# The returning products of the last two experts as seven products of 2x2 blocks

## The chip, the cores and the metric

The program runs on one core of one Trainium2 chip. The metric is the time of one execution on the device, in microseconds (us); less is better. All data is float32.

## The reference, cut to what matters

Two layers stand one behind the other. The first has a recurrent attention with a gated feed-forward part beside it; the second has a latent attention with 16 heads and a mixture of four experts beside it, and both parts of a layer add to its input `x`. The change touches the four experts alone:

```python
def _L1_ffn_ref(x, gate_up_proj, down_proj):      # x: 8 x 512 x 512 seen as 2048 rows of 512
    x4 = x.reshape(B, G, E, H)                    # E = 4: row j*4 + e goes to expert e
    gu = jnp.einsum('bgeh,ehd->bged', x4, gate_up_proj)
    gate, up = (gu[..., :I], gu[..., I:])
    inter = jax.nn.silu(gate) * up                # I = 512
    out = jnp.einsum('bgei,eih->bgeh', inter, down_proj)   # the returning product
    return out.reshape(B, N, H)
```

For each expert the returning product is a matrix of 512 tokens x 512 gated features times one of 512 x 512, added to the residual `y`.

## The kernel before, in words

The kernel has three parts in this order: the first layer (up to about 969 us of the profiled execution), the four experts (969 to 1135 us) and the latent attention (1135 us to the end). Each engine works through its own instructions in order. In the first and second part a scheduler sets that order from the program's dependences; instructions that go through `pin` (most of the attention's, and `fold`'s) keep the order in which they are written.

**Hidden products.** For each expert `hidden(e)` (L985) computes gate and up products. It already does so by seven products of 2x2 blocks: `right_sums(e)` (L947) makes four sums of the expert's tokens in the tile `t_ops` (four slots of 128x512), `left_sums` (L955) three sums of the weights in the tile `s_ops` and one in the weights' own place; the products are matmuls 256 columns wide (L969) into the PSUM tiles `epg` and `epu`, ScalarE copies partial results into `hold`, and the gated result goes to the tile `inter` (L1018), 128 x 4 x 512: gated features on the partitions, four chunks of them, by 512 tokens.

**Returning products.** `returned(e)` (L1024) takes, for each of four batches of 128 tokens, four matmuls of 128x512 (one for each chunk of gated features) into one PSUM bank `epo` of the pool `psp` (two banks), and VectorE adds the bank to `y` (L1039). The weights are the tile `dn`, loaded by `downs` (L921) through SyncE's queue while the expert before is returned. The order is: `hidden(1)`, `returned(0)`, `hidden(2)`, `returned(1)`, `hidden(3)`, `returned(2)` (L1062), `returned(3)` (L1082). Between them, in the second and third of these, the scheduler sets the preparation of the attention's first weights (`fold`, L850).

**What follows.** The attention's first instructions are the key and query products of its first head, `pk` (L1116) and `pq` (L1124), in the PSUM pool `ps_pj` (L1090), which takes over the experts' banks. Then ScalarE adds the bias, VectorE turns the vectors (`rotate`, L1094, instructions of L1099 and L1105) and GpSimd ends the turning (L1109); only then come the scores (L1134).

**The shared tiles.** `s_ops` and `t_ops` live through experts and attention. The attention's output product is by seven block products as well; its right sums (`right_operands`, L1219, four instructions of GpSimd on L1222 to L1225) are written to `t_ops`. In GpSimd's queue they stand ahead of two loads of rows of `W_O` (L859) and of all instructions of L1109.

**A matmul in the trace.** A float32 matmul shows as two records, so the 32 matmuls of 128x512 of `returned(2)` and `returned(3)` are 64 records, and they overlap: a record's duration is longer than the distance between two of them.

Of the kernel before, what the change touches and what calls it, by code (L numbers as in the profile page):

```python
# [12 lines left out]
F32 = mybir.dt.float32  # L13
# [5 lines left out]
P = 128  # L19
# [32 lines left out]
E, EI = 4, 512  # L52
# [3 lines left out]
def trunk_kernel(ctx: ExitStack, tc: tile.TileContext, a: dict, out: bass.AP):  # L56
    nc = tc.nc
# [48 lines left out]
    with ExitStack() as px:  # L106
# [303 lines left out]
        def queries_out(n, wh):  # L410

            po = ps_st.tile([P, NC, 4, K + 1], F32, tag="pso", name=f"pso_{n}")
            for be in range(NC):
                for b, r in enumerate(quarters):
                    mm(po[r, be, :, :K], wh[:, 4 * b + be, :], wq_bd[:, 4 * b + be, :, HD:], be == 0, False)
            return po
# [364 lines left out]
        for n in range(NM):  # L781
            wh = weights_out(n)
            pz = first_product(n, pre)
            po = queries_out(n, wh)
# [25 lines left out]
    y = [ypool.tile([P, E, HS], F32, tag=f"y{b}", name=f"y{b}") for b in range(B)]  # L810
    lat = ctx.enter_context(tc.tile_pool(name="lat", bufs=1, reuse_waits="tile"))
    ckv = lat.tile([P, B, L], F32, tag="ckv", name="ckv")
    s_ops = lat.tile([P, 3, 2, L // 2], F32, tag="s_ops", name="s_ops")
    t_ops = lat.tile([P, 4, 2, HS // 2], F32, tag="t_ops", name="t_ops")
# [24 lines left out]
    def batch_latents(hg, b):  # L839
        t = lat.tile([P, QC // P, L], F32, tag="cq", name=f"cq_{hg}_{b}", bufs=2)  # L840
        for i in range(QC // P):
            nc.sync.dma_start(out=t[:, i], in_=lat_d[1 + i][:, b].rearrange("p k x -> p (k x)"))
        return t

    def group_tiles(pool, hg):
        w = {nm: pool.tile([P, HPG, D], F32, tag=nm, name=f"{nm}_{hg}", bufs=1) for nm in ups}
        w["vo"] = pool.tile([P, HPG, HS], F32, tag="vo", name=f"vo_{hg}", bufs=1)
        return w
# [53 lines left out]
    with ExitStack() as px:  # L902
# [4 lines left out]
        psp = px.enter_context(tc.tile_pool(name="d_ps", bufs=2, space=PSUM))  # L907
        ps_gu = px.enter_context(tc.tile_pool(name="d_psgu", bufs=2, space=PSUM))
# [3 lines left out]
        def fetch(**kw):  # L912

            tc.keep_in_program_order(nc.sync.dma_start(**kw))
# [6 lines left out]
        def downs(e):  # L921
            dn = wd.tile([P, EI // P, HS], F32, tag="dn", name=f"dn_{e}")
            fetch(out=dn, in_=a["dn"][e].rearrange("(c p) o -> p c o", p=P))
            return dn
# [10 lines left out]
        dns = {0: downs(0)}  # L935
# [3 lines left out]
        half = B * P // 2  # L939
# [3 lines left out]
        def tokens(e, c, h):  # L943

            return xe[:, NCHUNK * h : NCHUNK * (h + 1), 2 * c : 2 * c + 2, e, :].rearrange("p k c j -> p c k j")

        def right_sums(e):  # L947
            t1, t2, t3, t4 = (t_ops[:, n].rearrange("p c (k j) -> p c k j", k=NCHUNK) for n in range(4))
            b22 = tokens(e, 1, 1)
            nc.vector.tensor_sub(t1, tokens(e, 0, 1), tokens(e, 0, 0))  # L950
            nc.vector.tensor_sub(t2, b22, t1)
            nc.vector.tensor_sub(t3, b22, tokens(e, 0, 1))
            nc.vector.tensor_sub(t4, tokens(e, 1, 0), t2)
# [29 lines left out]
        inters = {}  # L983
# [40 lines left out]
        def returned(e):  # L1024

            dn, inter = dns.pop(e), inters.pop(e)
            if e + 1 < E:
                dns[e + 1] = downs(e + 1)
            for b in range(B):
                po = psp.tile([P, HS], F32, tag="po", name=f"epo_{e}_{b}")  # L1030
                for i in range(EI // P):
                    nc.tensor.matmul(  # L1032
                        po,
                        lhsT=inter[:, i, b * P : (b + 1) * P],
                        rhs=dn[:, i, :],
                        start=(i == 0),
                        stop=(i == EI // P - 1),
                    )
                nc.vector.tensor_add(y[b][:, e, :], po, y[b][:, e, :])  # L1039

        right_sums(0)
        for e in range(E):
            if e == 1:
                nc.gpsimd.memset(ones, 1.0)
                nc.sync.dma_start(out=wqr, in_=a["W_QR"])
                nc.sync.dma_start(out=wkr, in_=a["W_KR"])
                buv16 = wk.tile([H, D], F32, tag="sg", name="buv16")
                nc.sync.dma_start(out=buv16, in_=a["b_UV"].rearrange("(h d) -> h d", d=D))
                w0 = group_tiles(lat, 0)
                cqs = {(0, 0): batch_latents(0, 0)}  # L1050
                first = fold(w0, 0, wk, lambda nm: psp.tile([P, 512], F32, tag="pa", name=nm), 1)
                nc.sync.dma_start(out=buk, in_=a["b_UK"])
                nc.sync.dma_start(out=buq, in_=a["b_UQ"])
                for k in range(E):
                    nc.sync.dma_start(
                        out=trig_k[RD:, :].rearrange("p (k e j) -> p k e j", k=NCHUNK, e=E)[:, :, k],
                        in_=a["trig"][:, k * P : (k + 1) * P].rearrange("p (k j) -> p k j", k=NCHUNK),
                    )
                nc.sync.dma_start(out=ckv, in_=lat_d[0].rearrange("p b k x -> p b (k x)"))
            hidden(e)  # L1060
            if e > 0:
                returned(e - 1)  # L1062
            if e in (1, 2):
                next(first, None)
            if e == 2:

                for wr, bias in ((wkr, buk), (wqr, buq)):
                    pb = psp.tile([P, 512], F32, tag="pa", name="pb")
                    nc.tensor.matmul(pb[RD:, :H], lhsT=wr, rhs=bias, start=True, stop=True)
                    nc.vector.tensor_copy(bias[RD:, :], pb[RD:, :H])  # L1070
                pb = psp.tile([P, 512], F32, tag="pa", name="pbuv")
                nc.tensor.transpose(pb[:, :H], buv16, ident[:H, :H])
                nc.vector.tensor_copy(buv, pb[:, :H])
                nc.vector.tensor_scalar_mul(buq[:RD, :], buq[:RD, :], scale)
                tc.keep_in_program_order(nc.vector.tensor_scalar_mul(trig_q[RD:, :], trig_k[RD:, :], scale))
            if e == 2:
                for b in range(B):
                    pt = psp.tile([P, E, P], F32, tag="pa", name=f"lv_tr_{b}")
                    for k in range(E):
                        nc.tensor.transpose(pt[:, k, :], ckv[:, b, k * P : (k + 1) * P], ident)  # L1080
                    nc.scalar.copy(lv[:, b], pt)
        returned(E - 1)  # L1082

# [2 lines left out]
    with ExitStack() as px:  # L1088
# [123 lines left out]
        half = L // 2  # L1212
# [109 lines left out]
        for i in range(nu + 1):  # L1322
# [37 lines left out]
            k = i - (nu - HPG * B)  # L1360
            if 0 <= k < HPG * B:
                b, e = divmod(k, HPG)
# [4 lines left out]
        po = {}  # L1367
# [106 lines left out]
```

## Time and profile before

| what | us |
|---|---|
| three executions, timed | 2035.77, 2028.45, 2035.72 |
| their median | 2035.72 |
| the profiled execution, its own time | 2030.29 |
| its span, first to last instruction | 2028.3 |
| TensorE busy in the span | 1968.2 (97%) |
| VectorE, ScalarE, GpSimd busy | 1302.3, 863.2, 631.8 |
| from the last hidden products of the last expert to the attention's first product, 1106.0 to 1135.5 | 29.5, of it TensorE 28.72, VectorE 7.91, ScalarE 1.01, GpSimd 4.02 |
| the 64 records of `returned(2)` and `returned(3)` in it, first and last start | 1106.23, 1134.1 |

The three timed executions lie 7.3 us apart, and the profiled one lies between them. About 2 us of its own time lie around its span.

In the profile's rows PE is TensorE, PEld its weight loads, DVE VectorE, ACT ScalarE, POOL GpSimd, and SPq the queue of SyncE. A row of the timeline gives the start in us, the time from the first start to the last end, the engine, the line, the operation, the tile written and those read, the shape, and in brackets how long the engine sat idle before it and what ended that. Rows of equal instructions that follow each other are merged (x62).

### The profile page before, as it was taken

The page shows a single profiled execution, that of the slowest core. Times are in us where ns is not written, and L with a number is a line of the kernel's source. Part 1 is how long each engine was busy: PE and PEld are TensorE (multiplying, and loading weights), DVE is VectorE, ACT ScalarE, POOL GpSimd, SP SyncE. Part 2 cuts the span into 40 slices and gives each one's busy share as a digit, 9 for nine tenths or more (in the row PEclk, how much of TensorE's full clock was granted, in tenths as well). Part 3 has the DMA queues.
Part 4 walks back from the last instruction along what each step waited for, and adds up shares of the span by engine and source line. Part 5 has one row for each costly group of instructions (what it writes and reads, how often), then busy time and mean ns, then how long its engine had stood idle before and what let it go on. Part 6 is the DMA issues. An engine that isn't in the chain of part 4 may idle for free.

```text
span 2028.3 us, 30787 instructions
## 1 busy us (share of the span) xinstructions
PE 1968.2 (97%) x10502; PEld 1245.2 (61%) x10502; DVE 1302.3 (64%) x2720; ACT 863.2 (43%) x1763; POOL 631.8 (31%) x707
## 2 busy tenths in 40 slices
PE   8999999999999999998999999999999999999999
PEld 6777676767676776744776445555555555555555
DVE  4546657575756574754654487777777777777773
ACT  2233343333343443422322365555555555555552
POOL 4334242434342433421001132223223232354320
PEclk9999999999999999999999999999999999999999
DMA  6757576646373655545831144344434443333332
GB/s 166 210 129 220 132 193 166 183 128 184 114 203 116 179 151 163 182 136 189 281 104 56 39 101 117 95 103 115 108 94 114 103 114 86 97 97 89 94 100 93
DMA packets 318472, 270.90 MB, mean 134 GB/s; under 512 B 87660, under 2 KB 239405, under 8 KB 317677
## 3 DMA queue, kind: packets, MB, share of 16 engines
q1 hardware_dynamic: 298080, 237.31, 43.2%
q0 software_dynamic: 8736, 26.31, 4.5%
q10 hardware_dynamic: 11500, 5.32, 0.9%
q8 instruction: 84, 1.38, 0.3%
q14 instruction: 72, 0.58, 0.1%
HBM read 174.18 MB, written 34.87 MB: 103 GB/s over the span
## 4 chain that ended last, share of the span: by engine, by line
PE 47%; DVE 1%; SPq 1%; ACT 1%; issue 0%; DMA 0%; DVEq 0%; ACTq 0%
PE sc L1134 9%; PE pc L1202 9%; PE pq L1124 7%; PE px L1245 5%; PE p L1245 4%; PE epg L969 3%; PE epo L1032 3%; PE pk L1116 2%; PE epu L969 1%; SPq L1194 1%; PE po L1302 1%; PE pw L868 1%; PE pvo L886 1%; ACT prob L1139 1%; ACT prob L1144 0%
## 5 line engine op out<-in xcount | busy, mean ns | idle before, releaser
L1139 ACT ACTIVATE prob<-sc,mx 128x512 f32<-128x512 f32 x256 | 174.3, 683 | 164.2 <-DVE mx L1136 159.4
L1134 PE MATMUL sc<-kT,qT 96*128 96x512 f32 x512 | 230.6, 592 | 1.6 <-DVE prT_head L1183 1.3
L1202 PE MATMUL pc<-prT,lv 128*128 128x512 f32 x488 | 219.6, 593 | 1.2 <-DMA prT<-tt 1.2
L1109 POOL TENSOR_TENSOR kT<-t_k,t_k 32x512 f32<-32x512 f32 x64 | 80.6, 1259 | 407.6 <-PE pq L1124 235.6
L1163 DVE STREAM_TRANSPOSE tt<-prob 128x512 f32<-128x512 f32 x248 | 170.3, 706 | 55.2 <-ACT prob L1144 43.7
L117 PE MATMUL pf<-xT,wg 128*128 128x256 f32 x704 | 173.7, 388 | 5.3 <-DMA wg<-in_wg 2.7
L1144 ACT ACTIVATE prob<-prob,sm 128x512 f32<-128x512 f32 x256 | 176.5, 713 | 0.0
L1124 PE MATMUL pq<-cq,uq 128*128 128x512 f32 x384 | 175.3, 592 | 0.8 <-ACT ctxT L1204 0.8
L1134 PEld LDWEIGHTS sc<-kT,qT 96*128 96x128 f32 x512 | 96.8, 190 | 124.1 <-issue 118.9
L1136 DVE TENSOR_REDUCE mx<-sc 128x1 f32<-128x512 f32 x256 | 168.0, 677 | 2.3 <-PE sc L1134 0.3
L117 PE MATMUL pf<-xT,wu 128*128 128x256 f32 x704 | 167.0, 380 | 1.3 <-DMA wu<-in_wu 1.3
L117 PE MATMUL pd<-wd,hid 128*128 128x512 f32 x352 | 165.9, 600 | 1.8 <-DMA wd<-in_wd 1.7
L117 PEld LDWEIGHTS pf<-xT,wg 128*128 128x128 f32 x704 | 132.1, 192 | 32.9 <-issue 7.6
L1202 PEld LDWEIGHTS pc<-prT,lv 128*128 128x128 f32 x488 | 92.5, 190 | 93.7 <-issue 90.7
L117 PEld LDWEIGHTS pf<-xT,wu 128*128 128x128 f32 x704 | 133.7, 190 | 20.4 <-DMA wu<-in_wu 2.3
L478 DVE SCALAR_TENSOR_TENSOR hid<-pf,us,sg 128x256 f32<-128x256 f32 x88 | 41.9, 477 | 153.9 <-ACT sg L477 153.5
L1124 PEld LDWEIGHTS pq<-cq,uq 128*128 128x128 f32 x384 | 72.8, 190 | 93.1 <-issue 81.5
L314 POOL TENSOR_SCALAR sk<-k,m 128x256 f32<-128x256 f32 x64 | 61.1, 964 | 179.8 <-PE pz L117 167.7
L421 POOL TENSOR_SCALAR gh<-grad,m 128x256 f32<-128x256 f32 x64 | 61.2, 967 | 153.2 <-DVE grad L390 135.5
L117 PEld LDWEIGHTS pd<-wd,hid 128*128 128x128 f32 x352 | 63.4, 190 | 60.5 <-issue 45.2
L1109 POOL TENSOR_TENSOR qT<-t_q,t_q 32x512 f32<-32x512 f32 x64 | 80.6, 1260 | 56.7 <-DVE t_q L1105 56.6
L477 ACT ACTIVATE sg<-pf,gs 128x256 f32<-128x256 f32 x88 | 41.5, 473 | 132.9 <-PE pf L117 132.5
(304 smaller groups left out, 3546.6 us busy)
## 6 DMA issues: line engine op xcount, KB each, us to landing
prT<-tt SPq DMA_DIRECT2D x992, 64.0 KB, 2.0
wd<-in_wd SPq DMA_DIRECT2D x176, 256.0 KB, 3.0
wg<-in_wg SPq DMA_DIRECT2D x88, 256.0 KB, 3.1
wu<-in_wu SPq DMA_DIRECT2D x88, 256.0 KB, 3.1
cq<-lat_d SPq DMA_DIRECT2D x48, 256.0 KB, 4.3
rows<-rows SPq DMA_DIRECT2D x128, 66.0 KB, 2.2
kv<-rows POOLq DMA_DIRECT2D x32, 264.0 KB, 4.1
gu<-in_gu SPq DMA_DIRECT2D x3, 2048.0 KB, 8.8
```

The lines of the kernel that those rows point to most:

```text
L117: nc.tensor.matmul(out, lhsT=lhsT, rhs=rhs, start=start, stop=stop, skip_group_check=True)
L421: nc.gpsimd.tensor_scalar_mul(gh[:, :, h, :], g, m2[:, h : h + 1])
L969: nc.tensor.matmul(ps, lhsT=w[:, c, :], rhs=x[:, c], start=start and c == 0, stop=c == 1, skip_group_check=True)
L1109: nc.gpsimd.tensor_sub(t[RD:mid, :], t1[RD:mid, :], t2[RD:mid, :])
L1124: nc.tensor.matmul(pq, lhsT=w[f"uq{i}"][:, h, :], rhs=cqs[hg, b][:, i, :], start=(i == 0), stop=(i == nq - 1))
L1134: pin(nc.tensor.matmul(ps, lhsT=qT[:KQ, i * P : (i + 1) * P], rhs=kT[:KQ, :], start=True, stop=True))
L1136: pin(nc.vector.tensor_reduce(mx, ps, AX.X, ALU.max, negate=True))
L1139: pin(nc.scalar.activation(pr, ps, AF.Exp, bias=mx, scale=1.0, accum_out=sm))
L1144: pin(nc.scalar.mul(pr, pr, sm))
L1163: nc.vector.transpose(out=tt[:, :, :, i, :], in_=pr.rearrange("p (kb e j) -> p kb e j", e=2, j=K))
L1202: pin(nc.tensor.matmul(pc, lhsT=lv[:, b, k, :], rhs=prT[:, k, :], start=(k == 0), stop=(k == E - 1)))
L1245: nc.tensor.matmul(ps[:, q, :], lhsT=a[:, k, q * P : (q + 1) * P], rhs=w[:, k, :], start=start and k == 0 and q == 0, stop=k == 1, skip_gr ...
```

## The change

For the experts 2 and 3 `returned` gives way to a new function; the experts 0 and 1 keep the old one. With the gated features cut in two halves (k) and the tokens and the output columns in two halves each, the product of two 2x2 block matrices is made with seven block products instead of eight, at the price of eight sums of blocks before them. Each block product is four matmuls, 256 columns wide. Four of the seven gather in one bank `x`, which VectorE reads between two of them, since the partial sums there are outputs themselves.

```diff
+        def returned_by_blocks(e):
+            dn, inter = dns.pop(e), inters.pop(e)
+            if e + 1 < E:
+                dns[e + 1] = downs(e + 1)
+            a11, a12, a21, a22 = (inter[:, 2 * k : 2 * k + 2, q * half : (q + 1) * half] for q in range(2) for k in range(2))
+            b11, b12, b21, b22 = (dn[:, 2 * k : 2 * k + 2, o : o + half] for k in range(2) for o in (0, half))
+            s1, s2, s4 = (s_ops[:, n] for n in range(3))
+            t1, t2, t3, t4 = (t_ops[:, n] for n in range(4))
+            nc.vector.tensor_sub(t1, b12, b11)
+            nc.vector.tensor_sub(t2, b22, t1)
+            nc.vector.tensor_add(s1, a21, a22)
+            nc.vector.tensor_sub(s2, s1, a11)
+            nc.vector.tensor_sub(t3, b22, b12)
+            nc.vector.tensor_sub(a21, a11, a21)
+            nc.vector.tensor_sub(s4, a12, s2)
+            nc.vector.tensor_sub(t4, b21, t2)
+
+            def product(ps, w, x, start=True):
+                for k in range(2):
+                    for q in range(2):
+                        nc.tensor.matmul(
+                            ps[:, q, :],
+                            lhsT=w[:, k, q * P : (q + 1) * P],
+                            rhs=x[:, k, :],
+                            start=start and k == 0 and q == 0,
+                            stop=k == 1,
+                            skip_group_check=True,
+                        )
+
+            def add(ps, qh, oh):
+                for q in range(2):
+                    t = y[2 * qh + q][:, e, oh * half : (oh + 1) * half]
+                    nc.vector.tensor_add(t, ps[:, q, :], t)
+
+            def bank(nm):
+                return psp.tile([P, 2, half], F32, tag="po", name=f"{nm}_{e}")
+
+            x = ps_gu.tile([P, 2, half], F32, tag="pg", name=f"eox_{e}")
+            product(x, a11, b11)
+            add(x, 0, 0)
+            p2 = bank("eo2")
+            product(p2, a12, b21)
+            product(x, s2, t2, False)
+            add(p2, 0, 0)
+            add(x, 0, 1)
+            p5 = bank("eo5")
+            product(p5, s1, t1)
+            product(x, a21, t3, False)
+            add(p5, 0, 1)
+            add(p5, 1, 1)
+            add(x, 1, 1)
+            p3 = bank("eo3")
+            product(p3, s4, b22)
+            product(x, a22, t4, False)
+            add(p3, 0, 1)
+            add(x, 1, 0)
...
             if e > 0:
-                returned(e - 1)
+                (returned if e < E - 1 else returned_by_blocks)(e - 1)
...
-        returned(E - 1)
+        returned_by_blocks(E - 1)
```

The sums are VectorE's, 128x512 each; they use the tiles that the hidden products and, later, the attention's output use: `s_ops`, `t_ops` and, for `a21`, the expert's own `inter`. The bank `x` is one of the hidden products' two `epg` banks; the other three products share the two `epo` banks.

## Prediction

> **What bounds the kernel now.** I read the page first, then the busy times by stage, then the timelines of TensorE, VectorE and GpSimd around the two returning products. The page says that TensorE bounds the whole:
>
> ```profile
> PE 1968.2 (97%) x10502; PEld 1245.2 (61%) x10502; DVE 1302.3 (64%) x2720; ACT 863.2 (43%) x1763; POOL 631.8 (31%) x707
> ```
>
> The stage of the change, by the windows (TensorE, weight loads, VectorE, ScalarE, GpSimd, then clock and DMA):
>
> ```profile
> 1107.95:1135.51 27.56, 26.77 (x64) 11.59 (x62) 6.79 (x12) 0.63 (x1) 2.31 (x3) 1.00 0.22 63
> ```
>
> TensorE is without a pause at full clock (1.00); VectorE has 6.79 us of work in 27.56. What ends here is TensorE's row, and one hand-over behind it. TensorE's timeline:
>
> ```profile
> 1104.40 1.13 PE L969 MATMUL epu<-xe,s_ops 128*128 128x256 f32 x4
> 1105.37 1.03 PE L969 MATMUL epg<-t_ops,gu 128*128 128x256 f32 x4
> 1106.23 1.02 PE L1032 MATMUL epo<-dn,inter 128*128 128x512 f32 x2
> 1107.09 1.03 PE L969 MATMUL epg<-t_ops,gu 128*128 128x256 f32 x4
> 1107.95 26.77 PE L1032 MATMUL epo<-dn,inter 128*128 128x512 f32 x62
> 1135.51 1.12 PE L1116 MATMUL pk<-ckv,uk 128*128 128x512 f32 x2 [0.79 <-DVE y L1039]
> ```
>
> Four records of 256 columns start 0.86 us before the next group (1105.37 to 1106.23), so 0.2155 us each; 62 of 512 columns give (26.77 - 0.592) / 61 = 0.429 each (0.592 is one record's mean). The last line shows the hand-over: `pk` waits for VectorE's last addition. VectorE's timeline there, and three of its rows elsewhere:
>
> ```profile
> 1058.59 0.69 DVE L950 TENSOR_TENSOR t_ops<-xe 128x512 f32<-128x512 f32 x1
> 1059.19 0.42 DVE L961 TENSOR_TENSOR s_ops<-gu 128x256 f32<-128x256 f32 x1
> 1059.53 0.69 DVE L951 TENSOR_TENSOR t_ops<-xe,t_ops 128x512 f32<-128x512 f32 x1
> ...
> 1134.76 0.69 DVE L1039 TENSOR_TENSOR y<-epo,y 128x512 f32<-128x512 f32 x1 [2.74 <-PE epo L1032]
> ```
>
> A sum of 128x512 lasts 0.69 us, but the next starts 0.60 behind it (1058.59, 1059.19); one of 128x256 lasts 0.42, the next starts 0.34 behind (1059.19, 1059.53). A result is read 0.20 us after TensorE's slot ends (slots end at 1107.95 + 62 x 0.429 = 1134.56, the addition starts at 1134.76), and TensorE starts 0.06 after an addition's end (1135.45, 1135.51).
>
> **The change part by part.**
>
> *TensorE.* Removed: 32 matmuls of 128x512, 64 records x 0.429 = 27.47 us. Added: 2 experts x 7 products x 4 matmuls = 56 of 128x256, 112 records x 0.2155 = 24.14 us. Gain 3.33 us. The price of 0.2155 is that of the same shape with its own weight load (190 ns) for each record, as in the hidden products. Nothing else of TensorE's is in the stretch, so the gain counts in full unless TensorE has to wait.
>
> *The last hand-over.* Before, `pk` starts 0.95 us after the last slot (1134.56 to 1135.51). In the built program of the changed kernel it waits for the additions of `eo3` of the last expert, and four matmuls (1.72 us) into `x` stand behind those products. Addition ready after 0.20 + 0.34 + 0.42 + 0.06 = 1.02 us: hidden with 0.70 to spare. Gain 0.95 us; if the cover went, it would cost what it cost before.
>
> *The sums and additions.* Removed from VectorE: 8 additions of 128x512. Added: 16 sums of 128x512 and 28 additions of 128x256. At the distances above, 16 x 0.60 + 28 x 0.34 = 19.1 us in a stretch of 24.1, so VectorE is at 80% and can make TensorE wait. I walked the built program's order through with these distances, from TensorE's slot at 1105.37 and VectorE free at 1103.81. `t1` and `s1` start when the last hidden products have read `t_ops` and `s_ops` (1103.54 + 0.20); the sums of expert 2 stand among the last operations of `hidden(3)` and end at 1109.7. TensorE needs none of them before it has done a11·b11, the last hidden product and a12·b21, at 1110.54; then it takes half of s1·t1, and at 1111.40 it is to add to `x`, which VectorE must have read by then:
>
> | TensorE comes to `x` for | at | VectorE is through with it | to spare |
> |---|---|---|---|
> | expert 2, s2·t2 | 1111.40 | 1111.13 | 0.27 |
> | expert 2, a21·t3 | 1114.42 | 1114.15 | 0.27 |
> | expert 2, a22·t4 | 1117.87 | 1117.57 | 0.30 |
> | expert 3, s2·t2 | 1123.47 | 1123.42 | 0.05 |
> | expert 3, a21·t3 | 1126.49 | 1126.22 | 0.27 |
> | expert 3, a22·t4 | 1129.51 | 1129.23 | 0.28 |
>
> Between two products into `x` the scheduler has put three other matmuls (1.29 us) or more, against the 1.02 that a reading takes, so where VectorE is free the pause is covered. The first and the fourth line are queues of VectorE: all eight sums of expert 2 stand ahead of the first reading, and six of expert 3 between the additions ahead of the fourth, where only 0.05 is left. Sum: no wait, `pk` at 1131.23 in place of 1135.51, **4.28 us** less. Cost of the sums from both sides: nothing, as walked (less is excluded: they are added work, and nothing late is taken away with them); and with every VectorE instruction taking its whole duration (0.69, 0.42) the same walk gives waits of 1.04, 0.30 and 1.08 us, together 2.4, and a gain of 1.9. I take nothing, since back-to-back rows show the shorter distance.
>
> [...]
>
> *GpSimd.* The attention's four sums into `t_ops` (L1222 to L1225, 1103.84 to 1109.53 before) now wait for the last expert's products: the first for s1·t1 (1126.1), the last for the last product (1131.4), so it ends at 1132.7. Behind it in the queue are two loads of `W_O` (1.09 us together, to 1133.8) and the turning of the first keys, which VectorE releases at 1139.16 - 4.28 = 1134.9. About 1.0 us to spare; gone, each further us delays the first scores. That move also takes these sums away from VectorE's: before, an operation with two SBUF inputs took 1.13 us beside one of them,
>
> ```profile
> 1106.48 1.27 POOL L1224 TENSOR_TENSOR t_ops<-vo 128x512 f32<-128x512 f32 x1
> ```
> ```profile
> 1106.89 1.13 DVE L1014 TENSOR_TENSOR hold<-hold 128x256 f32<-128x256 f32 x1 [0.83 <-ACT hold L1007]
> ```
>
> against 0.42 elsewhere. The eight sums of each expert have two SBUF inputs, too, but the last of them ends at 1122.7, ahead of GpSimd's first. So I cost this at nothing.
>
> *The rest.* `inter_3` is finished 0.7 us later (1110.7, 1110.0 before); its first reader is a sum at 1116.2 and SyncE's load of `cq` behind it (1110.11 to 1111.1) is wanted by products behind 1165. SyncE's load of `uq` for the next group waits for the last product as it did. `dn` of expert 3 was asked for at 1089.24. None is on the path.
>
> *Behind the stage.* Everything up to the first scores hangs from `pk`; the second half of the kernel has TensorE busy 841.69 of 848.30 us after 1180. An earlier start there is an earlier end. Sum against the profiled execution: 2030.29 - 4.28 = 2026.0. The median of the runs is 5.4 higher, so for the median 2035.72 - 4.3 = **2031.4 us**, which I give.
>
> **The rivals.**
>
> 1. *VectorE gives half of it back.* Whole durations instead of distances, with the waits above at the first and fourth line of the table. For it: 0.05 us to spare, and readings of PSUM in a row of 128x256 additions, which the trace of before does not have. Against: L1018's two in a row start 0.34 apart (1109.28, 1109.62), and two additions of 128x512 from PSUM in the attention (L1266, 0.65 us each) take 1.25 us together, 0.60 apart. Gain 1.9: 2028.4, for the median 2033.8. Chance 0.14.
> 2. *VectorE becomes the bound: slower.* The place is the same two lines. If besides whole durations every instruction took another 0.12 us for its semaphores, and each hand-over 0.1 more at TensorE and 0.04 at VectorE, the walk gives waits of 7.1 us and `pk` at 1138.3, 2.8 later than before: 2033.1, for the median 2038.5. It turns into a loss from about 0.055 us above the whole duration on. Against: rows that follow one another without another engine's wait lie at most 0.46 apart where one lasts 0.42 (L961 at 1089.93, L963 at 1090.39), 0.04 above the duration. Chance 0.07.
> 3. *It does not reach the end.* The time is won, but the start of the attention waits for something else: GpSimd's queue (1.0 us to spare) or the first transposed probabilities, for which `pc` waited 1.20 us on a DMA at 1176.85. For a full loss GpSimd would have to be 5.3 us late. 2030.3, for the median 2035.7. Chance 0.09.
>
> **How the numbers follow.** The forecast has 0.70. A measurement of this kernel tells about 0.5% (10 us) from no change; no case here moves it that much, and only the spread of the runs (2028.45 to 2035.77) can: a median from the low end, 2028.45 - 4.3 = 2024.2, would be 0.57% under 2035.72. I give 0.08 to faster by over 0.5%, 0.89 to within, 0.03 to slower. The range takes the forecast and rivals 1 and 3 on either end of that spread, 2024.2 to 2035.8, and one us beyond for runs outside the few shown: 2023 to 2037; rival 2 lies above it.
>
> **What would show it.** Right: 112 records of 0.38 us at distances of 0.2155 without idle time before the additions to `x`; `pk` without a wait for VectorE, 25.9 us after the hidden products that start at 1105.37 here (30.1 before); four GpSimd sums ending about 1.5 us after the last product. Wrong: idle time of TensorE put down to `y` before the second or fifth product into `x` (rival 1 or 2), rows of 128x256 additions further apart than 0.34, scores that wait for GpSimd, or a later stage that is longer by what this one is shorter (rival 3).

## The result, and the profile after

| | before | after |
|---|---|---|
| timed executions | 20 | 20 |
| median (lowest to highest), us | 2034.2 (2028.45 to 2035.77) | 2029.4 (2026.23 to 2034.58) |
| ratio of after to before | | 0.9981, 95% interval 0.9973 to 0.9988 |
| profiled execution, own time (span), us | 2030.29 (2028.3) | 2033.11 (2031.2) |
| its first part, start to the experts' first product, us | 969.35 | 976.62 |
| from there to the first `pk`, us | 166.16 | 161.91 |
| from `pk` to the end, us | 892.79 | 892.67 |

The ratio is that of the means; on 2034.2 us it is a gain of 3.9 us (2.4 to 5.5), and the two medians lie 4.8 us apart. The 4.28 foretold lies inside that interval. The change is below 0.5% of the time, the case to which the prediction gave 0.89.

The two profiled executions say the opposite at first sight: that of after is 2.8 us longer. The split by parts tells why. The first layer, where both kernels have the same code, took 7.27 us more; the stage of the change took 4.25 less; what follows took the same. So no number below is read from a span. Each is the distance between two instructions that stand in both kernels: from the last hidden products that start at 1105.37 in before and at 1112.63 in after to the first `pk`. It was 30.14 and is 25.90, **4.24 us less**.

In the page's first row of after, TensorE has 48 records more (112 - 64) and VectorE 40 instructions and 16 us more (2720 and 1302.3 before):

```profile
PE 1970.7 (97%) x10550; PEld 1258.7 (62%) x10550; DVE 1318.6 (65%) x2760; ACT 863.1 (42%) x1763; POOL 631.4 (31%) x707
```

The busy times of after for the stretch that answers to 1107.95 to 1135.51 in before (TensorE, weight loads, VectorE, ScalarE, GpSimd, then clock and DMA):

```profile
1115.21:1138.53 23.32, 23.32 (x109) 20.44 (x108) 17.85 (x44) 0.63 (x1) 3.76 (x3) 1.00 0.18 52
```

TensorE fills its stretch without a gap, though VectorE's 6.79 us of 27.56 have become 17.85 of 23.32. TensorE's timeline of after, beginning, middle and end:

```profile
1112.63 1.03 PE L969 MATMUL epg<-t_ops,gu 128*128 128x256 f32 x4
...
1130.76 1.90 PE L1062 MATMUL eox<-t_ops,s_ops 128*128 128x256 f32 x8
...
1136.81 1.89 PE L1062 MATMUL eox<-t_ops,inter 128*128 128x256 f32 x8
1138.53 1.02 PE L1174 MATMUL pk<-ckv,uk 128*128 128x512 f32 x2
```

No row ends in a bracket: neither the product that waits for the fourth reading of `x` (1130.76, fourth line of the prediction's table, with 0.05 us to spare there) nor `pk` waited. Eight records take 1.72 us (1136.81 to 1138.53), 0.215 each. VectorE's timeline of after, first the start of expert 2's sums, then the fourth reading:

```profile
1111.07 0.69 DVE L1050 TENSOR_TENSOR t_ops<-dn 128x512 f32<-128x512 f32 x1
1111.67 0.68 DVE L1052 TENSOR_TENSOR s_ops<-inter 128x512 f32<-128x512 f32 x1
...
1129.26 0.68 DVE L1057 TENSOR_TENSOR t_ops<-dn,t_ops 128x512 f32<-128x512 f32 x1
1129.86 0.74 DVE L1074 TENSOR_TENSOR y<-eox,y 128x256 f32<-128x256 f32 x2
1130.52 0.74 DVE L1074 TENSOR_TENSOR y<-eo,y 128x256 f32<-128x256 f32 x2
```

The starts lie 0.60 apart for a sum that lasts 0.69, and two additions of 0.41 are over in 0.74, so 0.33 apart: the distances that the prediction used for its walk through VectorE's queue. The walk, made in before's times, has `t1` start at 1103.81 and this reading at 1122.60; the trace has them 7.26 later each (1111.07, 1129.86), which is the lag that the stage began with (1112.63 - 1105.37). Nearly nineteen microseconds of queue came out to 0.01 us. The reading ends at 1130.60, TensorE could go on 0.06 later, and its product starts at 1130.76: 0.1 us was to spare.

GpSimd's last sum for the attention, after, and the turning of the first keys:

```profile
1138.84 1.27 POOL L1283 TENSOR_TENSOR t_ops<-vo,t_ops 128x512 f32<-128x512 f32 x1 [1.35 <-PE eox L1062]
...
1141.98 1.26 POOL L1167 TENSOR_TENSOR kT<-t_k,t_k 32x512 f32<-32x512 f32 x1 [0.84 <-DMA raw<-blocks_d]
```

The sum ends at 1140.11, 1.6 us behind the last product's slot; the turning starts at 1141.98, 3.45 us after `pk` (3.65 before). GpSimd sits idle for 0.84 us ahead of it, so the turning does not wait for the sums.

### The profile page after: what moved, and what is told of

It reads as the page before. It is cut to its first block, busy times and chain, and to the rows that moved or that the text cites. A ratio compares the mean times of both kernels' runs of the same rounds, so it can differ in the third digit from the quotient of the medians.

```text
span 2031.2 us, 30926 instructions
## 1 busy us (share of the span) xinstructions
PE 1970.7 (97%) x10550; PEld 1258.7 (62%) x10550; DVE 1318.6 (65%) x2760; ACT 863.1 (42%) x1763; POOL 631.4 (31%) x707
## 4 chain that ended last, share of the span: by engine, by line
PE 48%; DVE 2%; ACT 1%; SPq 0%; issue 0%; DMA 0%; DVEq 0%; ACTq 0%
PE pc L1260 10%; PE sc L1192 10%; PE pq L1182 8%; PE px L1303 5%; PE p L1303 4%; PE epg L969 3%; PE pk L1174 3%; PE epu L969 1%; PE epo L1032 1%; PE po L1360 1%; PE eox L1062 1%; PE pw L868 1%; PE pvo L886 1%; ACT prob L1197 1%; PE eo L1062 1%; SPq L1252 0%
```

## The experiments

Each was executed once, but for the one with all four experts (five times). A whole time of one execution says little beside a spread of seven microseconds, so they are judged by the distance from those last hidden products to `pk` (before 30.14, after 25.90). In none is a part of the computation left out or changed: what is doubled is done again into the same place. But the scheduler orders each version anew, and where another order than that of after bears on a reading, the text says so.

**The theory** is the prediction's: two terms, TensorE's slots and the last hand-over, with VectorE's sums and additions hidden. **The rivals** are that part of the gain is given back to VectorE, that VectorE becomes the bound, and that the time is lost behind the stage.

**One expert at a time.** The last alone:

```diff
-                (returned if e < E - 1 else returned_by_blocks)(e - 1)
+                returned(e - 1)
```

> Only the last expert is returned by blocks, expert 2 as before. Measured from the start of the hidden products that stand at 1105.37 us before and at 1112.63 after, to the first product of the attention (pk): 30.14 us before, 25.90 after. Theory (TensorE's slots, and the hand-over to pk that is covered by the last block products): 16 matmuls of 128x512 less 28 of 128x256 are 1.67 us, and the hand-over 0.95: 27.5 us, pk without a wait. Rival (the hand-over was not won by the change but by the profile's scatter): 28.5. Rival (VectorE's queue is what sets it, with whole durations): over 28.

and the third alone:

```diff
-        returned_by_blocks(E - 1)
+        returned(E - 1)
```

> Only expert 2 is returned by blocks, the last expert as before. The same distance (30.14 before, 25.90 after). Theory: 1.67 us of TensorE's slots are won, the hand-over of 0.95 stays, since pk waits again for the last addition of 128x512: 28.5 us with an idle of 0.8 before pk. Rival (the hand-over has nothing to do with which products stand last): 27.5, without that idle.

Measured: 27.55 and 28.49 us to `pk` (whole times 2031.37 and 2029.83). `pk` in the timelines of the last alone and of the third alone:

```profile
1136.61 1.02 PE L1174 MATMUL pk<-ckv,uk 128*128 128x512 f32 x2
```
```profile
1134.97 1.12 PE L1174 MATMUL pk<-ckv,uk 128*128 128x512 f32 x2 [0.78 <-DVE y L1039]
```

Expert 2 alone, the third, saves 1.65 (30.14 - 28.49), the last alone 2.59; together 4.24, which is what both save. An expert's slots are worth half of 3.33, and the last has 0.94 more, seen as the bracket in the second row: `pk` waits there for the old addition of 512 columns, and not in the first. The two terms stand apart and add up.

**Every sum twice.** Where does VectorE become the bound? Each of the eight sums but the one in place is issued twice:

```diff
             nc.vector.tensor_sub(t1, b12, b11)
+            nc.vector.tensor_sub(t1, b12, b11)
...
+            nc.vector.tensor_sub(t4, b21, t2)
             nc.vector.tensor_sub(t4, b21, t2)
```

> Each of the sums is made twice in a row, but for the one in place (7 of 8 for each expert): 14 more VectorE instructions of 128x512, 8.4 us at 0.60. Theory (VectorE has 0.05 us to spare ahead of the fourth reading of x and 0.27 ahead of the first, by its queue): TensorE waits about 1.3 us before the second product into x of expert 2, 4.3 us before that of expert 3 and 0.6 more; the distance is about 32.1 us, 2 us above before. Rival (VectorE at 80% has room, the sums lie beside TensorE's work): 25.9 to 27.

Measured: 35.95 us to `pk` (2046.83 whole). The direction is as expected, the size 3.8 more than the 32.1. TensorE's timeline has the waits at three readings:

```profile
1124.43 1.99 PE L1069 MATMUL eox<-t_ops,s_ops 128*128 128x256 f32 x8 [1.17 <-DVE y L1081]
...
1140.28 3.78 PE L1069 MATMUL eox<-t_ops,s_ops 128*128 128x256 f32 x8 [5.23 <-DVE y L1081]
...
1148.58 1.99 PE L1069 MATMUL eox<-t_ops,inter 128*128 128x256 f32 x8 [0.41 <-DVE y L1081]
```

A record's end lies about 0.16 us behind its slot (0.379 us a record, 0.2155 a slot), so the slots stood empty 1.33, 5.39 and 0.57; expected were about 1.3, 4.3 and 0.6. The first and last agree. (The last is no queue of VectorE, which had been idle: here two records stand ahead of that product, 0.43 us, and a reading takes 1.02.) The middle one is about 1.1 too long, and the timelines of GpSimd and VectorE have the reason:

```profile
1135.20 1.41 POOL L1287 TENSOR_TENSOR t_ops<-vo 128x512 f32<-128x512 f32 x1 [167.19 <-PE eo L1069]
```
```profile
1135.41 1.75 DVE L1059 TENSOR_TENSOR t_ops<-dn 128x512 f32<-128x512 f32 x1
```

With the queue so late, a sum of VectorE falls beside the first of GpSimd's: 1.75 us in place of 0.68, which is 1.07 of it. The other missing part is in the second row above: eight records last 3.78 us, not 1.99. The windows of that wait and the products behind it (the clock is the column before the last two):

```profile
1137.00:1138.60 1.60, 0.00 (x0) 0.00 (x0) 1.60 (x4) 0.00 (x0) 0.00 (x0) 0.95 0.00 0
1138.60:1140.20 1.60, 0.00 (x0) 0.00 (x0) 1.60 (x5) 0.00 (x0) 0.00 (x0) 0.50 0.01 5
1140.20:1142.00 1.80, 1.72 (x4) 1.45 (x5) 0.69 (x3) 0.00 (x0) 0.00 (x0) 0.50 0.00 0
```

TensorE's clock halved 3.4 us into the pause, at about 1138.4, and stayed so to about 1145.3 (from 1143.86 to 1145.85 its mean is 0.65). The eight records and the next six took 2.55 us more than their slots at full clock. 1.07 and 2.55 are 3.6 of the 3.8.

**The sums on GpSimd.** All eight go to the other engine:

```diff
-            nc.vector.tensor_sub(t1, b12, b11)
+            nc.gpsimd.tensor_sub(t1, b12, b11)
...
```

> All sixteen sums of the two experts are made by GpSimd (1.27 us each, as its own sums of 128x512) in place of VectorE (0.69). The distance from the last hidden products' slot to pk is 30.14 us before and 25.90 after. Theory (nothing of VectorE's work is on the path after the change, and GpSimd's sixteen sums, some 21 us, fit beside TensorE's 25.9): 25.9, no wait of TensorE. Rival (VectorE's operations with two SBUF inputs are held by GpSimd's, up to 1.3 us each for two of them in the gating of expert 3, and the sums come late): 26.5 to 29.

Measured: 26.33 us to `pk` (2036.69 whole, beside 2033.61 for before in one run), 0.43 more than after and so between theory and rival. TensorE has one wait, ahead of the first reading's product, and VectorE's timeline shows where it comes from:

```profile
1119.65 1.97 PE L1062 MATMUL eox<-t_ops,s_ops 128*128 128x256 f32 x8 [0.19 <-DVE y L1074]
```
```profile
1115.64 0.90 DVE L1014 TENSOR_TENSOR hold<-hold 128x256 f32<-128x256 f32 x1 [0.83 <-ACT hold L1007]
...
1118.44 0.73 DVE L1018 TENSOR_TENSOR inter<-hold,esg 128x256 f32<-128x256 f32 x1
1119.10 0.41 DVE L1074 TENSOR_TENSOR y<-eox,y 128x256 f32<-128x256 f32 x1
```

Two operations of the hidden products with both inputs in SBUF took 0.90 and 0.73 us beside GpSimd's sums (1114.99 to 1116.25 and 1117.62 to 1118.89), where they take 0.42 alone. The second stands ahead of the half of the reading that TensorE waits for (1119.10 to 1119.51). The collision is not the whole cause. After has four records of s1·t1 between a12·b21 and this product, and here the scheduler has put none, so TensorE comes 5.17 us behind the last hidden products' start instead of 6.04; the reading is through 5.39 behind it, 0.30 earlier than in after. At 0.42 in place of 0.73 the reading would just have been in time, and in the order of after it would have been so even with the collision. So the run shows that relieving VectorE brings nothing, and it doesn't show what the collision alone would cost.

**How much slack is there?** Only `t4` of the last expert is made again, two, nine and thirteen times in all:

```diff
-            nc.vector.tensor_sub(t4, b21, t2)
+            for _ in range(2 if e == E - 1 else 1):
+                nc.vector.tensor_sub(t4, b21, t2)
```

> The last sum of the last expert (t4) is made twice: one VectorE instruction of 128x512 more, 0.60 us, ahead of the fourth reading of x, where the walk leaves 0.05 us. Theory (VectorE's queue, by distances of 0.60 and 0.34): TensorE waits 0.6 us there, distance 26.45. Rival (there is more room than the walk says): 25.9. Rival (whole durations): 27 or more.

> The same sum nine times. By the walk, TensorE waits 2.1 us before the last product into x, distance 28.0; if GpSimd's first sum for the attention starts beside one of them, as in the run with all sums twice (1.75 us instead of 0.68), up to 1.1 more. Theory on the clock (in that run it was granted at half from about 3.4 us after TensorE had fallen idle): the idle time stays under 3.4, full clock, 28 to 29.1. Rival (any wait of TensorE of over 2 us halves it): 30 or more.

> The same sum thirteen times. By the walk TensorE waits 4.5 us before the last product into x, distance 30.4, with GpSimd's first sum beside it up to 31.5. Theory on the clock: over 3.4 us idle, so the products behind run at half clock for some us and the distance is 33 or more. Rival (the half clock in the run with all sums twice had another reason): 30.4 to 31.5 at full clock.

Measured: 26.58, 28.99 and 33.78 us to `pk` (2032.18, 2034.59 and 2035.18 whole). Made twice, the sum ends the stage 0.68 us later, where 0.55 was expected. That the numbers are close is luck, since neither the place nor the cause is the one expected. The scheduler has built another order on both engines: the second `t4` stands between the two halves of the fourth reading, and TensorE has eight records of s1·t1 ahead of that reading's product, where after has four. So nothing waits there. But only two records, in place of six, stand between the last two products into `x`. TensorE's and VectorE's timelines of twice:

```profile
1134.55 0.59 PE L1063 MATMUL eo<-dn,s_ops 128*128 128x256 f32 x2
1135.56 1.99 PE L1063 MATMUL eox<-t_ops,inter 128*128 128x256 f32 x8 [0.42 <-DVE y L1075]
```
```profile
1134.75 0.76 DVE L1075 TENSOR_TENSOR y<-eox,y 128x256 f32<-128x256 f32 x2 [0.94 <-PE eox L1063]
```

VectorE had been idle for 0.94 us when this reading came due, so its queue is not what TensorE waits for. The reading takes the 1.02 us of a hand-over, two records cover 0.43 of it, and the slots stood empty 0.58. How much slack VectorE's queue has is therefore not shown by these runs; the 0.1 us to spare in the trace of after is all that is known. Made nine and thirteen times, the order differs again: nothing stands between the last two products into `x`, and TensorE waits 0.62 us at an earlier product as well. What these two show is the clock behind a pause. Their rows of the last product into `x`:

```profile
1137.66 1.99 PE L1063 MATMUL eox<-t_ops,inter 128*128 128x256 f32 x8 [1.80 <-DVE y L1075]
```
```profile
1136.94 3.64 PE L1063 MATMUL eox<-t_ops,inter 128*128 128x256 f32 x8 [4.94 <-DVE t_ops L1058]
```

Behind a pause of 1.80 us the eight records last 1.99, as behind one of 0.42; behind 4.94 they last 3.64. The windows of thirteen times say the same with the clock:

```profile
1132.00:1136.90 4.90, 0.01 (x1) 0.00 (x0) 4.90 (x10) 0.00 (x0) 1.40 (x1) 1.00 0.00 0
1136.94:1140.42 3.48, 3.48 (x8) 2.82 (x9) 0.62 (x2) 0.00 (x0) 1.27 (x1) 0.51 0.00 0
```

The last product takes 3.48 us to `pk`, where it took 1.83 with nine times `t4`. So this wait is paid twice, once as a pause and once as half a clock (1.65 us) for what follows.

**All four experts.** The stage has the same products twice more. The right sums of the next expert's hidden products share `t_ops`, so their place is moved behind the returning products; for expert 0 they follow its hidden products:

```diff
-            if e + 1 < E:
-                right_sums(e + 1)
...
             hidden(e)
+            if e == 0:
+                right_sums(1)
             if e > 0:
-                (returned if e < E - 1 else returned_by_blocks)(e - 1)
+                returned_by_blocks(e - 1)
+                if e + 1 < E:
+                    right_sums(e + 1)
```

> All four experts are returned by blocks; for this the sums of the next expert's tokens, which use the same tiles, are moved behind the returning products. Measured from the first hidden product of expert 0 to pk: about 166.1 us before, 161.9 after. Theory: another 3.33 us of TensorE's slots, less what the first sums of the next expert make TensorE wait, once for each of two experts, 0 to 1 us each: 158.6 to 160.6; the time 2 us or so below that of the changed kernel. Rival (beside the preparation of the attention VectorE has no room, and the shared tiles put the sums on the path): 162 or more, no gain.

Measured: 2025.42 us median of 5 (2022.44 to 2027.07), beside 2034.12 for before (9 executions); ratio 0.9953, 95% interval 0.9940 to 0.9967, 9.6 us less (6.7 to 12.2), of which the stage shows 7.5. The stage from the experts' first product to `pk`:

```profile
972.24:1130.88 158.64, 156.61 (x735) 133.32 (x733) 112.61 (x272) 39.68 (x93) 3.77 (x3) 1.00 0.40 134
```

158.64 against 161.91 and 166.16: the first two experts give 3.27 more, again 1.64 each, and TensorE waits for nothing that it did not wait for in before. Its interval does not touch that of the change, so this version is ahead of both kernels.

## Why the prediction was right, point by point

- **TensorE's slots (3.33 us): right.** The single experts give 1.65 each, all four give 7.52 in the stage, where 2 x 3.33 + 0.95 would be 7.61. The price of 0.2155 held under products whose weights are loaded for each record.
- **The last hand-over (0.95 us): right.** 0.94, the difference of the two single experts. The cover is real: with `pk` behind products that do not depend on the last addition, its row has no bracket.
- **The sums and additions at nothing: right, by distances and not by durations.** Distances of 0.60 and 0.33 to 0.34 for 0.69 and 0.41. With whole durations the walk gave waits of 2.4 us in all; the trace has none. One count in this step was wrong: there are 32 additions of 128x256, not 28 (eight readings of two for each expert; the page's 40 more instructions are 16 + 32 - 8). At the same distances that is 16 x 0.60 + 32 x 0.34 = 20.5 us of 24.1, so the load is 85% and not 80% (in the trace VectorE is busy 17.85 of 23.32 us, 77%, since six of the sums start ahead of that stretch). The walk went by the built order, in which all 32 stand, and its times agree with the trace, so the result doesn't change. That TensorE waits nowhere hangs on 0.1 us at one place; what a little more work there would cost was not tried.
- **GpSimd's move at nothing: right in this kernel.** Its sums ended 1.6 us after the last product (about 1.5 foretold), and 0.84 us of idle time was left where about 1.0 was foretold. How thin the cover is shows where VectorE is late: a sum then falls beside GpSimd's, at 1.75 in place of 0.68 us.
- **The end moves with the stage: right.** 892.67 us behind `pk`, 892.79 before.
- **The time itself: near, by a base that moved.** 2031.4 was given and 2029.4 came out. The base was the median of three executions, 2035.72; that of twenty is 2034.2. The range of 2023 to 2037 would have held no gain at all as well, so the distances bear the mechanism, and the median alone doesn't.
- **Rival 1** (1.9 us of gain) lies outside the interval of 2.4 to 5.5, and TensorE has no idle time in the stage. **Rival 3** falls with the 892.67. **Rival 2**, whose added 0.12 us an instruction and 0.1 and 0.04 us a hand-over no trace shows, did not come true here, but VectorE does become the bound when the sums are doubled, and the stage is then 5.81 us longer than before. What was expected of that run was too low: it counted waits alone, and the clock behind them and the collision with GpSimd were 3.6 of 10.05 us over after.
- **What the prediction didn't see** is the sign of the profiled execution: it took that one's 2030.29 for a base to subtract from, and 2033.11 came out, since the first layer took 7.27 us more, with more of the clock lost (last section). The stage's distances show the cause, and the ratio over twenty executions agrees with them; the span of one execution shows neither.

That the gain in the whole time is 3.9 by the means and 4.8 by the medians, and not 4.24, is within the interval and needs no cause. What stays open is how much room VectorE's queue has, and how far lost clock makes the spread of the timed runs.

## What to carry to other kernels

A change of a few microseconds in a kernel whose runs lie seven apart is read as the distance between two instructions that both kernels have, on either side of the change, and not as a span; beside it, the parts before and behind must be shown to be the same. Count an engine's queue by the distance from start to start and walk it in the built order: with a queue loaded to 85%, durations and distances gave opposite answers (2.4 us of waits, or none). An instruction added as an experiment can change the order on other engines too: before a wait is put down to a queue, see whether the engine that it waits for had been idle. A wait of TensorE can cost more than itself in clock (4.94 us of pause and 1.65 more behind it, with `t4` thirteen times), and work moved to a second engine can lengthen the first one's instructions (0.90 us in place of 0.42, with the sums on GpSimd), so a rival in which an engine becomes the bound needs both on its bill.

## What the runs showed of the hardware that was not expected

**The same pause does or does not halve the clock.** In the first layer TensorE waits 2.72 us for GpSimd at the same place in both kernels. Timeline and windows of before, then of after:

```profile
263.60 0.48 PE L117 MATMUL pso<-a_bd,gh 128*32 128x68 f32 x17 [2.72 <-POOL gh L421]
```
```profile
263.60:271.00 7.40, 6.00 (x143) 5.05 (x144) 4.22 (x12) 3.57 (x7) 5.49 (x8) 1.00 0.72 187
```
```profile
266.17 0.48 PE L117 MATMUL pso<-a_bd,gh 128*32 128x68 f32 x17 [2.72 <-POOL gh L421]
```
```profile
266.20:273.60 7.40, 6.68 (x133) 5.22 (x134) 3.37 (x10) 2.72 (x6) 5.47 (x8) 0.55 0.73 190
```

The clock behind it is 1.00 in one and 0.55 in the other; in after it is half from 266.93 to 273.76. Ahead of the program's end these two traces have six stretches of half clock, of 3.41 us (before at 53.66 and 814.83, after at 55.30 and 929.12) or 6.83 us (after at 266.93 and 502.45). The two of before begin 761.17 us apart, the four of after 211.63, 235.52 and 426.67, which are 223, 62, 69 and 125 times 3.413. Laid on steps of that length, counted from these starts, the pause falls differently. In after it lies, but for its first 0.07 us, in one step (263.52 to 266.93), in which TensorE was busy for 0.76 us. In before it is split between two (from 258.45 and from 261.87), with 2.43 and 1.68 us busy. The same holds throughout both traces: between 20 and 2020 us TensorE was busy for 0.41 to 1.29 us in six of the steps, and a stretch of half clock begins behind each of them; in all others it was busy for 1.68 us or more, and none begins behind those. In after a pause of 3.06 us (821.59 to 824.65), split between steps with 1.70 and 2.06 us busy, has full clock behind it, and one of 2.39 us (51.80 to 54.19), all but its first 0.09 in a step with 1.11 us busy, has half. So where a pause falls on these steps went with the clock here, and not its length alone. What makes the steps is not shown.

Summed over the first 970 us (time times the missing share of the clock), before lost 3.4 us and after 10.2: 6.8 more, beside the 7.27 by which the first layer was longer. In the eight experiments the first 890 us alone lost 5.1 to 12.0 us (windows of 10 us), in steps of about 1.7. It isn't paid one for one: with `t4` thirteen times 11.9 us were lost there, and the first layer took 970.61 us, 1.3 more than in before. That it makes the spread of the timed runs is not shown. Only their mean clock is on record, and the longest of after (2034.58) has 0.995, the shortest (2026.23) 0.996.

**VectorE beside GpSimd.** Operations with both inputs in SBUF took 1.75 us (all sums twice, 1135.41), 1.68 (`t4` nine times, 1129.93), 0.90 and 0.73 us (sums on GpSimd, 1115.64 and 1118.44) beside one of GpSimd's where they take 0.68, 0.68, 0.42 and 0.42 alone; the additions with one input in PSUM stayed at 0.41 to 0.43 (the 32 into `y` in the run with the sums on GpSimd, 30 of them beside a sum of GpSimd's). In these four the price is 0.3 to 1.1 us an instruction; why the two kinds differ is not shown.
